# Evacuations one piece behind their products, B's additions on GpSimd, its transfers as single DMAs, and C's first sums in A's last rounds

**Chip, cores, metric.** One core of a Trainium2 chip. The metric is device time of one execution in microseconds (us); each quoted time is a median of several runs. The profile is of one such run. Engines: PE is TensorE, PEld its weight loads, DVE VectorE, ACT ScalarE, POOL GpSimd, SP the engine that issues the transfers.

## The reference

Four layers on x of shape 4 x 64 x 256 x 256, float32. Layers 0, 2 and 3 are long two-dimensional convolutions with a rank-one filter per channel; layer 1 goes to a Haar basis, mixes the channels, shrinks, and goes back.

```python
def _L0_conv_ref(x, ...):                       # also layers 2 and 3
    hx = _implicit_filter(z, Xw1, ...); hy = _implicit_filter(z, Yw1, ...)
    k = jnp.einsum('ijk,imk->ijmk', hx, hy)     # rank one: rows by columns
    y = irfft2(rfft2(x, 2L) * rfft2(k, 2L) / 2L)[..., :L, :L]
    return y + x * bias[:, None, None]

def _L1_conv_ref(x, v, conv_w, tau):
    f1 = haar2d(x)
    for i in range(2):
        f4 = jnp.einsum('bchw,oc->bohw', f1 * v[i], conv_w[i])
        acc = acc + jnp.sign(f4) * jax.nn.relu(jnp.abs(f4) - tau[i])
    return haar2d(acc, inverse=True) + x
```

## The kernel before

Because the filter has rank one, a convolution is two Toeplitz products (rows, then columns) on TensorE. The kernel has three phases, interleaved in program order:

- **A**: layer 0 and the forward Haar transform, 64 rounds of 12 pieces: 4 rows, 4 columns, 4 Haar products (of the round before). GpSimd does the sums of the other Haar direction. Results go to DRAM (`coef`).
- **B**: the mixing and shrinking, two groups of 128 units, each of three pieces (two units share one load of data); reads `coef`, `v`, `tau`, writes `mixed`. Group 0 lies beside the second half of A, group 1 beside the first half of C.
- **C**: the inverse Haar transform and layers 2 and 3, 64 rounds of 20 pieces.

Each engine works through its instructions in the order in which the pieces issue them. The parts that matter (cuts marked `...`):

```python
def rows(t, n):                                   # A; columns and product alike
    ps = bank(f"a1ps{n}_{t}")
    toeplitz(ps, s["x"][:, 2 * n : 2 * n + 2], s["toep"][n // NB], 0)
    s["y", n] = image("t0", f"ay{n}_{t}")
    nc.scalar.copy(s["y", n], ps)                 # evacuation, directly behind

# B: two PSUM pairs f4 in turn
def load(s):
    for g in range(2):                            # 64 partitions each
        part = slice(g * C, (g + 1) * C)
        nc.sync.dma_start(d["f"][part]..., coef[grp][:, rows]...)
        nc.sync.dma_start(d["v"][part]..., flat(v[rows]))
        nc.sync.dma_start(d["tau"][part]..., flat(taus[rows]))
def piece(u, j):
    if j == 0:   mix(u)              # PE     -> f4      (frees on threshold(u-2))
                 less(u - 1)         # DVE    |f4| - tau
    elif j == 1: multiply(u)         # DVE    f4 * v
                 sign(u)             # ACT
                 threshold(u - 1)    # DVE    max(., 0) * sign -> m, or -> f4 if u % 4 == 3
                 add(...)            # POOL   m + f;  then m + m on POOL, or m + f4 on DVE for odd s
    else:        magnitude(u)        # ACT

def beside(main, side, lead, tail):  # spreads the side pieces evenly, by number, over main
    ...
beside(a[:cut_a], rest, 2, 3 * M)              # rest: the filter networks of layers 2 and 3, ...
beside(a[cut_a:], phase_b(0), 5 * M, M)
beside(c[:cut_c], phase_b(1), 2 * M, 10 * M)   # C's first piece does the first loads and sums
beside(c[cut_c:], [], 0, 0)
```

## Time and profile before

3162.2 us (median of 4, 3160.7 to 3164.3). The prediction shows the busy times by stage, TensorE's floor in each and the waits. (A stage's floor is the time of its TensorE work at the full rate, as C shows it alone; what a stage takes beyond it is called lost.)

These lines of the page show who moves the data; the columns are the output and input, queue, count, KB of each, median us from issue to landing.

```profile
ft<-coef SPq DMA_DIRECT2D x256, 256.0 KB, 6.6
v<-in_v SPq DMA_DIRECT2D x256, 256.0 KB, 7.0
tau<-taus SPq DMA_DIRECT2D x256, 256.0 KB, 7.0
mixed<-gt SPq DMA_DIRECT2D x256, 256.0 KB, 6.0
```

Each of B's tensors takes two transfers of 64 partitions for every two units. These and the additions on two engines are what the change touches.

### The profile page before, as it was taken

The numbers are of one execution on the slowest core, as the hardware profiler recorded it, in microseconds if no ns is written. First come the engines' busy times: TensorE is split into PE (matmuls) and PEld (weight loads), VectorE is DVE, ScalarE is ACT, GpSimd is POOL, SyncE is SP. The second block draws the span as 40 slices with busy tenths as digits, with TensorE's granted clock in tenths as the row PEclk, the third lists the DMA queues.
The fourth block names the chain that finished last, engine by engine and source line by source line (L and its number), as shares of the span: only waits on it lengthen the run. The fifth ranks groups of instructions, "written<-read, shape, count | busy, mean of one in ns | idle before, by whom it ended". The sixth has DMA issues, their size and how long they took to land. (4 is left out here: it accounts for less than half of the span.)

```text
span 3159.3 us, 48195 instructions
## 1 busy us (share of the span) xinstructions
PE 2973.0 (94%) x17432; PEld 2535.1 (80%) x17432; DVE 1564.9 (50%) x1657; ACT 1230.2 (39%) x1799; POOL 1817.4 (58%) x2437
## 2 busy tenths in 40 slices
PE   5999999888988888599999999999999999999999
PEld 5989997666666666488877878887899999999998
DVE  2232213777777777457666667666732222222222
ACT  1333333444544445344444444444432222232222
POOL 2776675666766766655556555565664444444441
PEclk9999999999999999899999999999999999999999
DMA  6857898999999999789888988989744444444442
GB/s 159 215 179 193 226 234 226 258 274 272 274 275 270 274 277 265 230 195 268 233 244 226 250 231 238 249 226 255 205 141 132 141 124 124 124 138 132 127 120 87
DMA packets 380227, 656.76 MB, mean 208 GB/s; under 512 B 42134, under 2 KB 281399, under 8 KB 379992
## 3 DMA queue, kind: packets, MB, share of 16 engines
q1 hardware_dynamic: 379992, 653.69, 76.6%
q8 instruction: 140, 2.29, 0.3%
q14 instruction: 95, 0.78, 0.1%
HBM read 438.10 MB, written 215.42 MB: 207 GB/s over the span
## 5 line engine op out<-in xcount | busy, mean ns | idle before, releaser
L409 PE MATMUL f<-ft,mix_sb 128*128 128x512 f32 x1024 | 506.1, 617 | 112.6 <-DVE gt L438 57.3
L434 POOL TENSOR_TENSOR m<-m,ft 128x1024 f32<-128x1024 f32 x128 | 301.7, 2357 | 453.1 <-DVE m L429 441.4
L417 ACT ACTIVATE m<-f 128x1024 f32<-128x1024 f32 x256 | 262.5, 1025 | 513.1 <-DVE f L413 504.3
L546 DVE SCALAR_TENSOR_TENSOR cy<-cz,bias_sb,c1c 128x512 f32<-128x512 f32 x256 | 189.2, 746 | 515.9 <-PE c1c L224 515.9
L424 DVE TENSOR_TENSOR f<-f,tau 128x1024 f32<-128x1024 f32 x256 | 314.6, 1229 | 197.0 <-ACT f L420 194.2
L302 DVE SCALAR_TENSOR_TENSOR x<-x,bias_sb,a2ps 128x512 f32<-128x512 f32 x256 | 189.0, 745 | 428.8 <-PE a2ps L224 380.4
L409 PEld LDWEIGHTS f<-ft,mix_sb 128*128 128x128 f32 x1024 | 177.5, 193 | 258.3 <-issue 142.6
L546 DVE SCALAR_TENSOR_TENSOR o<-cy,bias_sb,c2c 128x512 f32<-128x512 f32 x256 | 189.5, 746 | 348.7 <-PE c2c L224 348.7
L413 DVE TENSOR_TENSOR f<-f,v 128x1024 f32<-128x1024 f32 x256 | 313.8, 1226 | 54.9 <-PE f L409 51.8
L223 PE MATMUL a1ps<-toep,x 128*128 128x256 f32 x1024 | 310.1, 385 | 21.3 <-DMA toep<-filt 18.1
L223 PE MATMUL a2ps<-toep,ay 128*128 128x256 f32 x1024 | 305.9, 381 | 1.8 <-ACT ay L292 1.8
L223 PE MATMUL c2r<-toep,cy 128*128 128x256 f32 x1024 | 305.8, 380 | 0.3 <-DVE cy L546 0.3
L223 PE MATMUL c1c<-toep,ch 128*128 128x256 f32 x1024 | 305.8, 380 | 0.0
L223 PE MATMUL c1r<-toep,cz 128*128 128x256 f32 x1024 | 305.8, 380 | 0.0
L223 PE MATMUL c2c<-toep,ch 128*128 128x256 f32 x1024 | 305.8, 380 | 0.0
L533 ACT COPY ch<-c2r 128x512 f32<-128x512 f32 x256 | 149.4, 588 | 382.4 <-PE c2r L224 382.2
L325 ACT ACTIVATE f<-a3ps,wcol_sb 128x512 f32<-128x512 f32 x256 | 175.7, 686 | 293.2 <-PE a3ps L317 251.5
L317 PEld LDWEIGHTS a3ps<-haarH_sb,fw 128*128 128x128 f32 x2048 | 244.9, 195 | 32.5 <-issue 22.7
L526 ACT COPY cz<-c1ps 128x512 f32<-128x512 f32 x256 | 148.1, 588 | 309.5 <-PE c1ps L522 309.5
L522 PEld LDWEIGHTS c1ps<-haarW_sb,ci 128*128 128x128 f32 x2048 | 238.8, 193 | 36.6 <-POOL ci L266 24.4
L522 PE MATMUL c1ps<-haarW_sb,ci 128*128 128x128 f32 x2048 | 244.6, 276 | 23.4 <-POOL ci L266 23.3
L420 ACT ACTIVATE f<-f 128x1024 f32<-128x1024 f32 x256 | 263.9, 1031 | 0.0
(64 smaller groups left out, 5868.5 us busy)
## 6 DMA issues: line engine op xcount, KB each, us to landing
toep<-filt SPq DMA_DIRECT2D x768, 128.0 KB, 4.1
x<-in_x SPq DMA_DIRECT2D x256, 256.0 KB, 7.8
coef<-f SPq DMA_DIRECT2D x128, 512.0 KB, 7.3
ft<-coef SPq DMA_DIRECT2D x256, 256.0 KB, 6.6
v<-in_v SPq DMA_DIRECT2D x256, 256.0 KB, 7.0
tau<-taus SPq DMA_DIRECT2D x256, 256.0 KB, 7.0
mixed<-gt SPq DMA_DIRECT2D x256, 256.0 KB, 6.0
g<-mixed SPq DMA_DIRECT2D x128, 512.0 KB, 5.4
```

What stands on the lines that cost most here:

```text
L223: nc.tensor.matmul(ps[:, m, :], data[:, 0, cut], t[:, which, :], start=True, stop=False)
L302: nc.vector.scalar_tensor_tensor(s["x1"][:, cut], s["x"][:, cut], bias_sb[:, c : c + 1], ps, ALU.mult, ALU.add)
L317: nc.tensor.matmul(ps[:, e, bass.ts(k, P)], s["fw"][:, 2 * (n + e) + k, bass.ts(m, P)], haarH_sb[:, k, :], start=True, stop=True,)
L325: nc.scalar.activation(f4[:, n : n + 2, m, :], ps, AF.Copy, scale=wcol_sb[:, m : m + 1])
L409: nc.tensor.matmul(un[u]["f4"][:, j, :], mix_sb[:, u % 2, :], f[:, j, :], start=True, stop=True)
L413: nc.vector.tensor_tensor(f4, f4, weights(st[u // 2]["v"], u % 2), ALU.mult)
L417: nc.scalar.activation(un[u]["m"], un[u]["f4"], AF.Sign)
L420: nc.scalar.activation(un[u]["f4"], un[u]["f4"], AF.Abs)
L424: nc.vector.tensor_tensor(f4, f4, weights(st[u // 2]["tau"], u % 2), ALU.subtract)
L434: nc.gpsimd.tensor_tensor(m0, m0, data(st[s]["f"]), ALU.add)
L522: nc.tensor.matmul(ps[:, m, bass.ts(h, P)], s["ci"][:, 2 * n + h, bass.ts(m, P)], haarW_sb, start=True, stop=True)
L546: nc.vector.scalar_tensor_tensor(o, s["y", n], bias_sb[:, at : at + 1], ps, ALU.mult, ALU.add)
```

## The change

Its intent: let no engine stand in front of an evacuation whose product is not done, take work and a PSUM wait off VectorE, move B's data in transfers of all 128 partitions, and fill the gap between A and C. Core of the diff (cut):

```diff
+    waiting = []
+    def later(op): waiting.append(op)
+    def flush():                    # called at the start of every piece of A and C
+        for op in waiting: op()
+        waiting.clear()
...
-            nc.scalar.copy(s["y", n], ps)
+            later(lambda: nc.scalar.copy(y, ps))          # the other five evacuations alike
...
-            for g in range(2): ... two DMAs of 64 partitions for f, v and tau each
+            nc.sync.dma_start(d["f"]..., rows_of(coef[grp], r0))   # partition = 2 * channel + g
+            for name, src in (("v", v), ("tau", taus)):
+                flat = bass.AP(src.tensor, ..., [[0, C], [C * 2 * W, 2], [1, ROWS * 2 * W]])
+                nc.sync.dma_start(d[name]..., flat)
...
-            o = un[u]["f4"] if u % 4 == 3 else un[u]["m"]
-            nc.vector.scalar_tensor_tensor(o, ...)
+            nc.vector.scalar_tensor_tensor(un[u]["m"], ...)
-                if s % 2: nc.vector.tensor_tensor(data(st[s]["g"]), m0, un[2 * s + 1]["f4"], ALU.add)
-                else:     nc.gpsimd.tensor_tensor(...)
+                nc.gpsimd.tensor_tensor(data(st[s]["g"]), m0, un[2 * s + 1]["m"], ALU.add)
...
-    beside(a[cut_a:], phase_b(0), 5 * M, M)
-    beside(c[:cut_c], phase_b(1), 2 * M, 10 * M)
+    beside(a[cut_a : -6 * M], phase_b(0), 5 * M, 0)           # B ends two rounds before A
+    beside(a[-6 * M : -2 * M], c_first[:1], 2 * M, M)         # C's first loads
+    beside(a[-2 * M :], c_first[1:], 0, 0)                    # C's first sums
+    main = a_last[:1] + c[:M]                                 # A's last sums; C's first products
+    for pair in zip(c[M : 2 * M], a_last[1:]): main += pair   # A's last products between C's rows
+    main += a_last[M + 1 :] + c[2 * M : cut_c]
+    beside(main, phase_b(1), 5 * M, 10 * M)
```

The mixing matrix and the fix of B's first row are rewritten for the new order of partitions.

More of the change, by code (lines that the diff above doesn't have):

```diff
@@ L68, in conv_haar_kernel @@
 def conv_haar_kernel(
-    ctx: ExitStack, tc: tile.TileContext, x, zT, w1, wbd, cols, decay, bias, haarW, haarH, wcol, wrow, mixT, v, tau, out
+    ctx: ExitStack, tc: tile.TileContext, x, zT, w1, wbd, cols, decay, bias, haarW, haarH, wcol, wrow, mixT, first, v, tau, out
 ):
@@ L198, in conv_haar_kernel @@
     mix_sb = const.tile([P, 2, P], F32, tag="mix", name="mix_sb")
-    nc.gpsimd.memset(mix_sb, 0.0)
-    for i in range(2):
-        for g in range(2):
-            s = slice(g * C, (g + 1) * C)
-            nc.sync.dma_start(mix_sb[s, i, s], mixT[i])
+    nc.sync.dma_start(mix_sb, mixT)
+    first_sb = const.tile([P, 2], F32, tag="first", name="first_sb")
+    nc.sync.dma_start(first_sb, first)
     def load_toeplitz(l, t, bufs):
@@ L269, in inverse_free, with later @@
             half *= 2
+    waiting = []
+    def later(op):
+        waiting.append(op)
+    def flush():
+        for op in waiting:
+            op()
+        waiting.clear()
     def run(ops, count):
@@ L290, in rows @@
             toeplitz(ps, s["x"][:, 2 * n : 2 * n + 2], s["toep"][n // NB], 0)
-            s["y", n] = image("t0", f"ay{n}_{t}")
-            nc.scalar.copy(s["y", n], ps)
+            y = s["y", n] = image("t0", f"ay{n}_{t}")
+            later(lambda: nc.scalar.copy(y, ps))
         def columns(t, n):
@@ L301, in columns @@
             cut = slice(2 * n, 2 * n + 2)
-            nc.vector.scalar_tensor_tensor(
-                s["x1"][:, cut], s["x"][:, cut], bias_sb[:, c : c + 1], ps, ALU.mult, ALU.add
+            later(
+                lambda: nc.vector.scalar_tensor_tensor(
+                    s["x1"][:, cut], s["x"][:, cut], bias_sb[:, c : c + 1], ps, ALU.mult, ALU.add
+                )
             )
@@ L324, in product @@
             f4 = s["f"].rearrange("p (n m) k -> p n m k", m=2)
-            nc.scalar.activation(f4[:, n : n + 2, m, :], ps, AF.Copy, scale=wcol_sb[:, m : m + 1])
+            dst = f4[:, n : n + 2, m, :]
+            later(lambda: nc.scalar.activation(dst, ps, AF.Copy, scale=wcol_sb[:, m : m + 1]))
         def coarsest(t):
@@ L342, in piece @@
         def piece(t, j):
-            now, last = t < total, t > 0
+            flush()
             if j == 0:
@@ L349, in piece @@
             if j < M:
-                if now:
-                    rows(t, j)
-                if last:
+                rows(t, j)
+                if t > 0:
                     run(st[t - 1]["ops"], 2)
             elif j < 2 * M:
-                if now:
-                    columns(t, j - M)
+                columns(t, j - M)
                 if j == M and t > 1:
@@ L361, in piece @@
             else:
-                if last:
+                if t > 0:
                     product(t - 1, j - 2 * M)
-                if now:
+                if t < total - 1:
                     run(st[t]["ops"], 2)
-        for t in range(total + 1):
+        for t in range(total):
             for j in range(3 * M):
                 pieces.append(lambda t=t, j=j: piece(t, j))
-        pieces.append(lambda: (coarsest(total - 1), store(total - 1)))
-        return pieces
+        t = total - 1
+        last = [lambda: (flush(), coarsest(t - 1), store(t - 1), run(st[t]["ops"], 16))]
+        last += [lambda j=j: (flush(), product(t, j)) for j in range(M)]
+        last.append(lambda: (flush(), coarsest(t), store(t)))
+        return pieces, last
     def phase_b(grp):
@@ L387, in load, with rows_of @@
             d["tau"] = bp.tile([P, ROWS, 2, W], F32, tag="tau", name=f"tau_{grp}_{s}", bufs=3)
-            for g in range(2):
-                part = slice(g * C, (g + 1) * C)
-                rows = slice(g * C + r0, g * C + r0 + ROWS)
-                flat = lambda ap: ap.rearrange("r i h k -> (r i h k)").partition_broadcast(C)
-                nc.sync.dma_start(
-                    d["f"][part].rearrange("p r b w -> p (r b w)"),
-                    coef[grp][:, rows].rearrange("c r b h k -> c (r b h k)"),
-                )
-                nc.sync.dma_start(d["v"][part].rearrange("p r i w -> p (r i w)"), flat(v[rows]))
-                nc.sync.dma_start(d["tau"][part].rearrange("p r i w -> p (r i w)"), flat(taus[rows]))
+            nc.sync.dma_start(d["f"].rearrange("p r b w -> p (r b w)"), rows_of(coef[grp], r0))
+            for name, src in (("v", v), ("tau", taus)):
+                flat = bass.AP(src.tensor, src.offset + r0 * 2 * W, [[0, C], [C * 2 * W, 2], [1, ROWS * 2 * W]])
+                nc.sync.dma_start(d[name].rearrange("p r i w -> p (r i w)"), flat)
+        def rows_of(ap, r0):
+            return ap.rearrange("c (g r) b h k -> c g r (b h k)", g=2)[:, :, r0 : r0 + ROWS].rearrange(
+                "c g r e -> c g (r e)"
+            )
         def data(t):
@@ L426, in threshold @@
         def threshold(u):
-            o = un[u]["f4"] if u % 4 == 3 else un[u]["m"]
-            nc.vector.scalar_tensor_tensor(o, un[u]["f4"], 0.0, un[u]["m"], ALU.max, ALU.mult)
+            nc.vector.scalar_tensor_tensor(un[u]["m"], un[u]["f4"], 0.0, un[u]["m"], ALU.max, ALU.mult)
         def add(s, which):
@@ L436, in add @@
                 st[s]["g"] = bp.tile([P, ROWS, NB, W], F32, tag="gt", name=f"gt_{grp}_{s}", bufs=3)
-                if s % 2:
-                    nc.vector.tensor_tensor(data(st[s]["g"]), m0, un[2 * s + 1]["f4"], ALU.add)
-                else:
-                    nc.gpsimd.tensor_tensor(data(st[s]["g"]), m0, un[2 * s + 1]["m"], ALU.add)
+                nc.gpsimd.tensor_tensor(data(st[s]["g"]), m0, un[2 * s + 1]["m"], ALU.add)
         def store(s):
@@ L445, in store @@
             if r0 == 0:
-                top = gt[:C, 0].rearrange("p b (h k) -> p b h k", h=2)
-                sd = bp.tile([C, NB, 2, N], F32, tag="sd", name=f"sd_{grp}", bufs=1)
-                nc.vector.tensor_tensor(sd[:, :, 0, :], top[:, :, 0, :], top[:, :, 1, :], ALU.add)
-                nc.vector.tensor_tensor(sd[:, :, 1, :], top[:, :, 0, :], top[:, :, 1, :], ALU.subtract)
-                nc.vector.tensor_copy(top, sd)
-            for g in range(2):
-                part = slice(g * C, (g + 1) * C)
-                rows = slice(g * C + r0, g * C + r0 + ROWS)
-                nc.sync.dma_start(
-                    mixed[grp][:, rows].rearrange("c r b h k -> c (r b h k)"), gt[part].rearrange("p r b w -> p (r b w)")
-                )
+                top, low = (gt[:, 0].rearrange("p b (h k) -> p b h k", h=2)[:, :, h, :] for h in range(2))
+                d = bp.tile([P, NB, N], F32, tag="sd", name=f"sd_{grp}", bufs=1)
+                one, sign_ = first_sb[:, 0:1], first_sb[:, 1:2]
+                nc.vector.tensor_scalar(d, top, one, None, ALU.mult)
+                nc.vector.scalar_tensor_tensor(top, low, one, top, ALU.mult, ALU.add)
+                nc.vector.scalar_tensor_tensor(low, low, sign_, d, ALU.mult, ALU.add)
+            nc.sync.dma_start(rows_of(mixed[grp], r0), gt.rearrange("p r b w -> p (r b w)"))
             st[s].clear()
@@ L524, in product @@
                     )
-            s["y", n] = image("t0", f"cz{n}_{t}")
-            nc.scalar.copy(s["y", n], ps)
+            y = s["y", n] = image("t0", f"cz{n}_{t}")
+            later(lambda: nc.scalar.copy(y, ps))
         def rows(t, l, n):
@@ L531, in rows @@
             toeplitz(ps, s["y", n], s["toep"][l - 1][n // NB], 0)
-            s["half", n] = image("t1", f"ch{l}{n}_{t}")
-            nc.scalar.copy(s["half", n], ps)
+            y = s["half", n] = image("t1", f"ch{l}{n}_{t}")
+            later(lambda: nc.scalar.copy(y, ps))
         def columns(t, l, n):
@@ L545, in columns @@
                 o = image("t2", f"cy{n}_{t}")
-            nc.vector.scalar_tensor_tensor(o, s["y", n], bias_sb[:, at : at + 1], ps, ALU.mult, ALU.add)
+            old = s["y", n]
+            later(lambda: nc.vector.scalar_tensor_tensor(o, old, bias_sb[:, at : at + 1], ps, ALU.mult, ALU.add))
             s["y", n] = o
@@ L556, in piece @@
         def piece(t, j):
+            flush()
             stage, n = divmod(j, M)
             if j == 0:
-                if t == 0:
-                    load(0)
-                    load(1)
-                    sums(0)
-                    run(st[0]["ops"], 16)
-                    filters(0)
                 filters(t + 1)
@@ L577, in piece, with start @@
                 run(st[t + 1]["ops"], 1)
+        def start():
+            load(0)
+            load(1)
+            filters(0)
+            sums(0)
+        first = [start] + [lambda: run(st[0]["ops"], 2)] * 8
         for t in range(total):
@@ L581, in phase_c @@
                 pieces.append(lambda t=t, j=j: piece(t, j))
-        pieces.append(lambda: store(total - 1))
-        return pieces
+        pieces.append(lambda: (flush(), store(total - 1)))
+        return first, pieces
     def beside(main, side, lead, tail):
@@ L593, in beside @@
             done = max(done, want)
-    a, c = phase_a(), phase_c()
+    (a, a_last), (c_first, c) = phase_a(), phase_c()
     cut_a, cut_c = ROUNDS * 3 * M, ROUNDS * 5 * M
@@ L600, in conv_haar_kernel @@
     bps = pool("bps", 2, space=PSUM)
-    beside(a[cut_a:], phase_b(0), 5 * M, M)
-    beside(c[:cut_c], phase_b(1), 2 * M, 10 * M)
+    beside(a[cut_a : -6 * M], phase_b(0), 5 * M, 0)
+    beside(a[-6 * M : -2 * M], c_first[:1], 2 * M, M)
+    beside(a[-2 * M :], c_first[1:], 0, 0)
+    main = a_last[:1] + c[:M]
+    for pair in zip(c[M : 2 * M], a_last[1:]):
+        main += pair
+    main += a_last[M + 1 :] + c[2 * M : cut_c]
+    beside(main, phase_b(1), 5 * M, 10 * M)
     beside(c[cut_c:], [], 0, 0)
@@ L662 @@
     haarW[0] *= math.sqrt(0.5)
+    mix = np.zeros((C, 2, 2, C, 2), np.float32)
+    for g in range(2):
+        mix[:, g, :, :, g] = a["L1_conv_conv_w"].transpose(2, 0, 1)
+    odd = np.arange(P) % 2
     arrays = {
@@ L690 @@
         "wrow": f(w[order].astype(np.float32)),
-        "mixT": f(a["L1_conv_conv_w"].transpose(0, 2, 1)),
+        "mixT": f(mix.reshape(P, 2, P)),
+        "first": f(np.stack([1.0 - odd, 2.0 * odd - 1.0], axis=1).astype(np.float32)),
         "v": by_row(v),
```

## The prediction

> **What bounds the kernel now.** I read, in this order, the page's busy shares, the busy time by stage (cut at 37 us, where the first product starts; at 522, where B's first load is issued; at 1321, A's last product; at 1343, C's first; at 2371, 32 rounds of C before the end), the waits of TensorE inside the stages, then the timeline. Columns of the stage view: stretch, its us, busy us (instructions) of PE, PEld, DVE, ACT, POOL, then granted clock, DMA share, GB/s.
>
> ```profile
> PE 2973.0 (94%) x17432; PEld 2535.1 (80%) x17432; DVE 1564.9 (50%) x1657; ACT 1230.2 (39%) x1799; POOL 1817.4 (58%) x2437
> ...
> 37.00:522.00 485.00, 479.64 (x3231) 449.60 (x3231) 120.06 (x164) 169.11 (x268) 336.24 (x625) 1.00 0.78 213
> 522.00:1321.00 799.00, 689.07 (x3444) 517.02 (x3442) 574.18 (x539) 384.35 (x504) 531.78 (x685) 0.97 1.01 264
> 1321.00:1343.00 22.00, 0.09 (x1) 0.09 (x1) 0.00 (x0) 0.64 (x1) 11.96 (x21) 0.61 0.89 276
> 1343.00:2371.00 1028.00, 1014.59 (x5640) 834.38 (x5641) 670.43 (x675) 448.64 (x640) 597.08 (x624) 1.00 0.85 228
> 2371.00:3159.00 788.00, 784.39 (x5114) 731.63 (x5113) 191.30 (x257) 224.90 (x384) 339.86 (x480) 1.00 0.42 125
> ```
>
> TensorE bounds it, so I need its floor per piece. In the chain of waits C's second half repeats with a period of 24.53 us a round: 32 Haar products take 3.57 us, and each pair of Toeplitz products (256 and 128 columns) 0.655 us, 32 of them 20.96. So an A round (rows, columns, product) has a floor of 5.24 + 5.24 + 3.57 = 14.05 us, and one of B's 256 units (two mixing products in four records) 1.72 us. Whole floor: 64 x 14.05 + 64 x 24.53 + 256 x 1.72 = 2909 us.
>
> Stage by stage: A alone until 522 is 33.67 rounds less one product, floor 469, took 485. A with B's first group: the rest of A (430) and 128 units (220), floor 650, took 799: **149 us lost**. The hand-over from A to C: 22 us with TensorE empty. C with B's second group: 785 + 220 = 1005, took 1028: 23 lost. C alone: nothing lost. So this is about the second stage and the hand-over. Who is waited for there:
>
> ```profile
> PE f L409 <- DVE gt L438: 45.7, 29, 3.5
> PE f L409 <- DVE m L429: 35.0, 35, 2.7
> PE f L409 <- DMA ft<-coef: 4.2, 3, 1.6
> ```
>
> (560 to 1290 us; total us, times, longest.) TensorE waits almost only before B's mixing product: its two-bank PSUM pair is free when VectorE has thresholded the unit two before (L429), or, for every fourth unit, has added it (L438, in order behind GpSimd's first addition). The idle records give 110 of the 149 us; the rest I put down to the lower granted clock (0.97) and refilling after each gap. Why VectorE is late, from the timeline:
>
> ```profile
> 906.15 0.75 DVE L302 SCALAR_TENSOR_TENSOR x<-x,bias_sb,a2ps 128x512 f32<-128x512 f32 x1 [2.24 <-PE a2ps L224]
> 906.82 1.22 DVE L413 TENSOR_TENSOR f<-f,v 128x1024 f32<-128x1024 f32 x1
> 907.95 1.21 DVE L429 SCALAR_TENSOR_TENSOR m<-f,m 128x1024 f32<-128x1024 f32 x1
> ...
> 909.22 1.98 PE L409 MATMUL f<-ft,mix_sb 128*128 128x512 f32 x4 [1.79 <-DVE m L429]
> ```
>
> The multiplication's input was ready at about 904.8 (mixing product at 902.82, 1.98 long), yet VectorE sat 2.24 us in front of A's evacuation, which waited for its own product; TensorE then waited 1.79 us (PE's own record) for the threshold at the end of that queue. The evacuation blocks the queue just when VectorE has B's work to do.
>
> **What the Trainium skill says.** "PSUM — Partial Sum Buffer", section "Engine vs sequencer instructions": ScalarE's, VectorE's and GpSimd's queues are strict FIFO. The lines above agree: 2.24 us lost with a ready instruction behind. "SBUF — State Buffer", section "Door 1: The DMA port swizzle": partitions 0..63 or 64..127 alone reach 8 of 16 ports, with an asymptote of about 218 GB/s. The trace agrees: the packet records of B's first loads (64 partitions each) show about 315 ns per 4 KB, at 218 GB/s, against 159 ns for A's 128-partition stores just before.
>
> ```profile
> 524.00:550.00 26.00, 19.92 (x88) 14.34 (x89) 10.50 (x11) 8.96 (x12) 11.20 (x20) 0.87 1.04 218
> ```
>
> "GPSIMD Engine Reference", section "3.1 Elementwise": an addition is 1.96 times slower on GpSimd at 2048 elements; here 2357 ns against 1221 at 1024, a ratio of 1.93. "SBUF — State Buffer", section "SBUF: two separate sides": GpSimd shares a port lock with VectorE operations of two SBUF inputs. B's and the evacuations' VectorE operations take one input from PSUM, and GpSimd's addition stays between 2339 and 2378 ns, so I count no slowing from the moved additions.
>
> **The change part by part.**
>
> 1. *Evacuations one piece behind.* Count unchanged: VectorE 0.745 us, ScalarE 0.59 to 0.69 each. They reach the queue when their product is done, so the 2 us blockings go. What then limits a unit? In the new schedule B's 394 steps lie over 340 pieces of A, three steps a unit, so 2.59 pieces a unit: TensorE's period is 1.72 + 2.59 x 1.171 = 4.75 us on average, 5.1 beside rows or columns, 4.03 beside products. The dependency mix (1.97) -> multiply (1.23) -> threshold of the unit before (1.21) -> next mix runs in about 4.5 us (815.11 to 819.61 in the trace). It fits beside rows and columns, not beside products: 0.47 us x 1.55 units x 28.3 rounds = 21 us lost. Beside columns VectorE has 3.67 + 2.59 x 0.745 = 5.6 us a unit against 5.1: for a unit and a half per round, some 0.35 us x 28 = 10 us.
>
> 2. *Additions on GpSimd.* VectorE loses 64 x 1.221 = 78 us in all, GpSimd gains 64 x 2.357 = 151. The wait for L438 goes. GpSimd in the second stage then has 128 x 2.357 = 302, and 28.33 rounds of A's sums at 10.55 (the sum of the rows of L235 to L244 and L331 to L333 over 64) = 299: 601 us of a TensorE floor of 28.33 x 14.05 + 220 = 618. That is 97%, tight, but over a stage of some 650 it is 92%. Its lag builds up beside products (5.4 us a round by the same sums) and drains beside rows and columns; five buffers for m give three units, 14 us.
>
> 3. *Single DMAs.* Same bytes. With 16 ports they should go at 159 ns a packet. Off the path directly (few waits for data above), but B's first 24 loads took 29 us, so starting gets some 10 us better (I leave 5 of loss). It is also needed: 64 steps x 2.1 MB and 28.3 rounds x 2.62 MB are 208 MB, which in 654 us are 318 GB/s; the stage now runs at 271 with the DMA share at 1.04.
>
> 4. *C's first sums in A's last rounds.* The hand-over now costs the 22 us, and 9 more in A's last round:
>
> ```profile
> 1315.50 5.42 PE L317 MATMUL a3ps<-haarH_sb,fw 128*128 128x128 f32 x32 [9.02 <-POOL fw L235]
> 1342.91 5.37 PE L522 MATMUL c1ps<-haarW_sb,ci 128*128 128x128 f32 x32 [22.00 <-POOL ci L266]
> ```
>
> After: GpSimd still has C's first sums (11.7 us, rows of L264 and L266 over 64) and then A's last (10.5) in a row, while TensorE has 5.24 + 3.57 us before it needs the first and 3.57 + 1.31 more before it needs the second. With GpSimd about 3 us behind at the start I get waits of 6 and 6.5: 13 us in place of 31. B ends before A's last two rounds, which run at their floor, 28.
>
> 5. *Store's first row, the mixing matrix:* a few instructions of a microsecond; nothing.
>
> **The sum.** Start 37 + A alone 469 + 14 lost (as now, a little less) = 520. A with B: 618 + 21 + 10 + 5 = 654, to 1174. A's last two rounds: 29, to 1203. Hand-over waits 13, to 1216. C with B, with A's last product: 3.6 + 1005 + 8 lost (23 now; the same blocking is removed, the unit period of about 7.2 us is loose) = 1017, to 2233. C alone 785, last store 3: **3021 us**, 4.5% below 3161.6; I say 3020.
>
> **The rivals.**
> *GpSimd becomes the bound.* For: 97% of the floor, strict order, additions that wait for VectorE (131 us of waits for L429 between 560 and 1290). Against: those waits come from late thresholds, which part 1 brings forward. If 10% of the stage stays idle, it takes 667 to 670; if 15%, 707: 3035 to 3075.
> *The chain of B is the bound everywhere.* Latencies and interposed evacuations make a unit take 5.2 us instead of 4.75 on average: 131 x 5.2 = 681, 3050. For: only two PSUM pairs. Against: 4.5 us loops are seen.
> *The transfers become the bound.* If single DMAs gained nothing, 64 x 9.85 us (2.1 MB at 213 GB/s) plus 28.3 x 7 (2.62 MB at about 375, the best 5 us of the stage) would be 829 us: only the hand-over and C would gain, 3130 to 3195. Against: A's 128-partition stores already go at 159 ns.
> On the good side, with the whole stage at the floor of 618 and 5 of waits at the hand-over: 2980.
>
> **Range and chances.** The good side and the GpSimd rival span 2980 to 3075; 8 in 10 for 2985 to 3070. Faster by over 2% needs less than 3098: only the transfer rival, or two others together, prevents it: 0.93. Within 2%: 0.06. Slower: 0.01.
>
> **What would show it.** Right: between B's first load and A's last two rounds some 655 us; waits of the mixing product for VectorE down from 81 us to some 30, those left beside A's Haar products; no VectorE evacuation with 2 us of idle before it; GpSimd about 92% busy there and all 128 of B's second additions on it; packets of B's loads near 160 to 200 ns, over 300 GB/s; two waits on GpSimd of 5 to 8 us at the hand-over; C alone unchanged. Wrong: TensorE waiting for GpSimd's fw in every round, ScalarE's sign waiting for m (GpSimd's buffers), or waits for ft, v, tau (transfers).

## The result, and the profile after

3032.4 us (median of 4, 3030.3 to 3034.7) against 3162.2. The ratio is 0.9589, 95% interval 0.9573 to 0.9606. Here and below a ratio is the mean time of one kernel's fast runs over that of the other's of the same rounds, so not quite the ratio of the medians. The prediction was 3020, range 2985 to 3070.

First the busy shares of the page, then the stages of the kernel after, cut at the same events (531: B's first load; 1191: A's last two rounds begin; 1225: C's first product; 2244: C's second half):

```profile
PE 2949.6 (97%) x17432; PEld 2528.4 (83%) x17432; DVE 1489.4 (49%) x1593; ACT 1229.1 (41%) x1799; POOL 1968.6 (65%) x2500
...
35.00:531.00 496.00, 486.14 (x3232) 454.75 (x3232) 120.21 (x164) 169.31 (x268) 337.07 (x625) 0.99 0.76 209
531.00:1191.00 660.00, 632.05 (x3216) 475.75 (x3216) 527.12 (x499) 370.57 (x482) 575.29 (x660) 0.99 0.92 314
1191.00:1225.00 34.00, 28.45 (x196) 26.61 (x194) 5.97 (x8) 11.06 (x18) 31.34 (x55) 0.96 0.52 187
1225.00:2244.00 1019.00, 1012.94 (x5665) 836.87 (x5666) 635.10 (x642) 450.59 (x644) 684.27 (x679) 1.00 0.68 233
2244.00:3033.00 789.00, 785.14 (x5121) 732.42 (x5119) 192.09 (x257) 225.05 (x384) 340.40 (x480) 1.00 0.42 125
```

From B's first load to C's first product it was 821 us and is 694: the whole gain is there. C with B is 8 us shorter, A alone 10 us *longer*. Beside B's first group DMA runs at 314 GB/s with a share of 0.92, where it ran at 264 with 1.01. The waits of TensorE over the whole span (total us, times, longest):

```profile
PE f L424 <- DVE m L442: 25.3, 36, 3.6
...
PE c1ps L528 <- POOL ci L266: 5.7, 1, 5.7
PE a1ps L223 <- ACT f L339: 4.5, 1, 4.5
PE a2ps L223 <- ACT ay L303: 4.5, 2, 2.8
PE a3ps L330 <- POOL fw L235: 3.9, 2, 3.6
```

The wait for the addition's line is gone, that for the threshold has become small, and the hand-over is two waits (5.7, and 3.6 of the 3.9). The two lines with ACT, all before B's first load, are 9.0 us, where the kernel before had 5.0; the prediction did not have that. VectorE's evacuations beside B no longer wait for their product: between 531 and 1191 us the profile shows 0.8 us of such waits, where the kernel before had 65.7 between 560 and 1290.

### The profile page after: what moved, and what is told of

Same layout as the page of the kernel before. It is cut to its first block, busy times and chain, and to the rows that moved or that the text cites. A ratio compares the mean times of both kernels' runs of the same rounds, so it can differ in the third digit from the quotient of the medians.

```text
span 3032.9 us, 47710 instructions
## 1 busy us (share of the span) xinstructions
PE 2949.6 (97%) x17432; PEld 2528.4 (83%) x17432; DVE 1489.4 (49%) x1593; ACT 1229.1 (41%) x1799; POOL 1968.6 (65%) x2500
## 4 chain that ended last, share of the span: by engine, by line
PE 79%; DVE 5%; POOL 3%; issue 2%; DMA 2%; ACT 1%; SPq 0%; POOLq 0%; DVEq 0%; ACTq 0%
PE f L424 12%; PE c1c L223 7%; PE c1r L223 7%; PE c1ps L528 7%; PE c2r L223 7%; PE c2c L223 7%; PE a1ps L223 4%; PE a2ps L223 4%; PE c1c L224 4%; PE c1r L224 4%; PE c2r L224 4%; PE c2c L224 4%; PE a3ps L330 3%; PE a1ps L224 2%; DVE f L428 2%
## 5 line engine op out<-in xcount | busy, mean ns | idle before, releaser
L424 PE MATMUL f<-ft,mix_sb 128*128 128x512 f32 x1024 | 490.5, 601 | 29.1 <-DVE m L442 25.3
L450 POOL TENSOR_TENSOR gt<-m,m 128x1024 f32<-128x1024 f32 x128 | 302.8, 2365 | 177.2 <-DVE m L442 117.5
L442 DVE SCALAR_TENSOR_TENSOR m<-f,m 128x1024 f32<-128x1024 f32 x256 | 310.7, 1214 | 0.1
L264 POOL TENSOR_TENSOR i<-g 128x8 f32<-128x8 f32 x64 | 14.3, 223 | 389.3 <-DMA g<-mixed 389.3
L435 ACT ACTIVATE f<-f 128x1024 f32<-128x1024 f32 x256 | 263.2, 1028 | 0.0
```

The source lines that it names most:

```text
L424: nc.tensor.matmul(un[u]["f4"][:, j, :], mix_sb[:, u % 2, :], f[:, j, :], start=True, stop=True)
L435: nc.scalar.activation(un[u]["f4"], un[u]["f4"], AF.Abs)
L442: nc.vector.scalar_tensor_tensor(un[u]["m"], un[u]["f4"], 0.0, un[u]["m"], ALU.max, ALU.mult)
L450: nc.gpsimd.tensor_tensor(data(st[s]["g"]), m0, un[2 * s + 1]["m"], ALU.add)
```

## The experiments

Twelve kernels; all gave correct results. "Stage" is the time from B's first load to the start of A's last two rounds, 660 us in the changed kernel. The kernel before took 3164 to 3165 us in these lots. The changed kernel itself was not run in them, so differences of a few us from its 3032.4 are judged by the ratios.

| run | edit | us | ratio to before |
|---|---|---|---|
| (the change) | | 3032.4 | 0.9589 |
| after_evac_now | without the deferral | 3086.3 | 0.9754 |
| before_evac_later | the deferral alone | 3151.8 | 0.9967 |
| after_two_dmas | two half transfers, in turn | 3067.1 | 0.9698 |
| after_two_dmas_old_order | two half transfers, the old order | 3129.5 | 0.9884 |
| after_two_row_dmas | two full-width transfers | 3030.4 | 0.9566 |
| after_adds_dve | odd additions back on VectorE | 3077.0 | 0.9722 |
| after_old_handover | the old hand-over | 3031.9 | 0.9575 |
| after_old_handover_dense | the same, B packed as in the change | 3051.5 | 0.9638 |
| after_flush_mlp | evacuations ahead of the network | 3026.2 | 0.9553 |
| after_by_time | B's steps laid out by time | 3029.0 | 0.9565 |
| after_mlp_by_time | the last two together | 3021.7 | 0.9542 |
| after_old_handover_mlp_time | all three | 3024.1 | 0.9548 |

### Are the evacuations the cause?

`after_evac_now`: deferral undone in the changed kernel.

```diff
     def later(op):
-        waiting.append(op)
+        op()
```

> The changed kernel with the evacuations of A and C issued at once again, directly behind their products; all else as changed. Theory (the evacuations waiting for their own product block VectorE's and ScalarE's queues, and that was most of the 149 us lost beside B's first group): the stage between B's first load and A's last two rounds grows from 660 to 720 to 750 us, the time from 3032 to 3080 to 3115 us, and VectorE again shows evacuations with 2 us of idle in front of them. The stretch before B gets some 10 us shorter (the network's layers). Rival (the gain came from the moved additions and the single transfers): under 3050 us.

Measured 3086.3 us. The stage is 713 us, and A alone is 10 us shorter again. VectorE waits for A's column products (first line, 560 to 1180 us), and TensorE for the threshold (second line, whole span):

```profile
DVE x L314 <- PE a2ps L224: 44.8, 51, 1.6
...
PE f L424 <- DVE m L442: 72.2, 73, 4.1
```

So the deferral is worth 54 us of the final time, and the mechanism is the predicted one: with 45 us of VectorE in front of unfinished products, TensorE waits 47 us more in front of its PSUM pair. In size the expectation was too high: the stage was to be 720 to 750 us, the single wait 2 us, and the longest is 1.6.

`before_evac_later`: the same deferral put into the kernel before, nothing else (`later` and `flush` as in the diff above).

> The kernel before with the evacuations one piece behind, and nothing else of the change. Theory (evacuations are the main cause of the waits, but transfers of 64 partitions at half rate are a second lid just above): the transfers of the stage, 214 MB at the 275 to 280 GB/s that the kernel before reaches at best over 20 us or more, need about 765 to 780 us, so only 20 to 35 us come off the 799 us, and 10 us are lost in the stretch before B: 3135 to 3155 us, with waits for ft, v or tau showing up on TensorE or VectorE. Rival A (transfers are no lid): the stage falls to 700 to 720 us, 3080 to 3100 us. Rival B (evacuations do not matter): 3160 to 3175 us.

Measured 3151.8 us, only 12 less. TensorE now waits for data, from 560 to 1180 us:

```profile
560.00:1180.00 620.00, 531.29 (x2667) 399.11 (x2666) 448.78 (x421) 297.99 (x391) 413.74 (x525) 0.97 1.03 267
...
PE f L424 <- DMA ft<-coef: 52.6, 22, 5.4
PE f L424 <- DVE gt L453: 17.3, 17, 2.0
...
530.00:1338.00 808.00, 689.55 (x3441) 518.82 (x3440) 574.35 (x539) 383.12 (x503) 532.50 (x685) 0.96 1.01 262
1359.00:2371.00 1012.00, 1008.54 (x5635) 832.44 (x5636) 671.53 (x675) 448.19 (x640) 598.38 (x624) 1.00 0.86 231
```

The waits for `ft` were 4.2 us in a longer window of the kernel before. With the evacuations out of the way, the limit is the DMA engines, which at a share of 1.03 move 267 GB/s. The last two lines are A with B's first group (B's first load to A's last product) and C with the second. The profile is of the slowest of the four executions (3161.7 us, 10 above the median); but even without those 10 us the first of the two stretches would be as long as in the kernel before (799 us). Of the 20 to 35 us that I expected there nothing is seen; what the deferral alone gains lies in C (1012 us against 1028). So in this stage of the kernel before the transfers were a limit as near as VectorE, although few waits there name them. Rival A, that transfers are no lid, falls.

### Is it the transfers, and what about them?

`after_two_dmas`: each of B's transfers as two, partitions 0 to 63 and 64 to 127.

```diff
-            nc.sync.dma_start(d["f"]..., rows_of(coef[grp], r0))
+            for q in (0, 1):
+                cs, ps_ = slice(q * 32, q * 32 + 32), slice(q * C, q * C + C)
+                nc.sync.dma_start(d["f"][ps_]..., rows_of(coef[grp], r0)[cs])
 # v, tau and mixed alike, tensor by tensor
```

> The changed kernel with each of B's four transfers cut in two again, channels 0 to 31 (partitions 0 to 63) and 32 to 63 (partitions 64 to 127); layout, bytes and packets unchanged. Theory (half of the ports, half of the rate, which the faster stage can no longer bear): the stage goes from 660 to 740 to 770 us, DMA share over 1.0 at 270 to 280 GB/s, 4 KB packets near 315 ns, waits of TensorE for ft or of VectorE for v and tau, time 3110 to 3145 us. Rival (the transfers are hidden anyway, the single DMAs only tidy up): under 3045 us.

Measured 3067.1 us: a loss of 35, well under what I expected (the stage is 702 us, not 740 or more). TensorE waits 33 us for `ft`, but the stage moves 299 GB/s (560 to 1180 us), more than I allowed for. So in this order the halves do not cost what they cost in the kernel before. Its order was another: all tensors of one half, then all of the other.

`after_two_dmas_old_order`:

```diff
+            for q in (0, 1):            # q outermost: f, v, tau of one half, then of the other
+                nc.sync.dma_start(d["f"][ps_]..., rows_of(coef[grp], r0)[cs])
+                for name, src in (("v", v), ("tau", taus)):
+                    nc.sync.dma_start(d[name][ps_]..., flat)
```

> As the run with two transfers of 64 partitions each, but in the order of the kernel before: coefficients, v and tau of the first 64 partitions, then those of the other 64. Same number of transfers, same bytes. Theory (what counts is that all transfers in flight go to the same half of the ports): slower than the alternating order, which took 3067 us: 3080 to 3130 us, 4 KB packets near 300 ns, DMA share at 1.03 or more with 270 to 290 GB/s in the stage. Rival (the number of transfers or their issue counts): the same as the alternating order, 3060 to 3072 us.

Measured 3129.5 us, 97 more than the change (stage 760 us), with the same number of transfers as the run before it. The upper lines are the old order's stage and its wait for data over the whole span; below them B's first loads, before A's transfers mix in, in the single form (533 to 547 us of the changed kernel):

```profile
560.00:1180.00 620.00, 549.79 (x2648) 405.05 (x2646) 443.77 (x417) 308.62 (x400) 478.25 (x546) 0.95 1.04 277
...
PE f L425 <- DMA ft<-coef: 65.8, 23, 5.1
```

```profile
533.00:547.00 14.00, 12.67 (x61) 9.24 (x62) 6.71 (x6) 6.52 (x9) 8.88 (x16) 1.00 0.99 360
```

`after_two_row_dmas`: two transfers again, but all 128 partitions in each, cut along the row.

```diff
+            for q in (0, 1):
+                e = slice(q * W, q * W + W)
+                nc.sync.dma_start(d["f"]...[:, e], rows_of(coef[grp], r0)[:, :, e])
```

> The changed kernel with each of B's transfers cut in two along the row and not along the partitions: 128 partitions each, 2 KB packets, same bytes, twice the number of transfers and issues. Theory (ports, not number): 3028 to 3042 us, as the changed kernel. Rival (number of transfers or the time to issue them): 3055 to 3075 us, as with two transfers of 64 partitions.

Measured 3030.4 us, the same as the change. So it is not that there are fewer transfers, or that they take less time to issue: it is that each covers all 128 partitions. (Each packet here has 2 KB and takes a median of 84 ns in the first loads, so 4 KB take about as long as in one transfer.) The packet records of B's first loads agree: 4 KB take a median of 159 ns in the changed kernel and 315 in the old order of halves, and the rate is 360 against 223 GB/s. In those first loads the alternating halves reach 232 GB/s, 4% more than the old order; the Trainium skill, "SBUF — State Buffer", section "Can I just issue two DMAs to hit both halves?", measured 6% for two such transfers at once, which is close. Why alternating then costs 35 us and the old order 97 is not settled. Between 560 and 1180 us, where A's transfers run beside B's, the 4 KB packets take a median of 180 ns with alternation, 238 in the old order and 159 in the changed kernel, so there the two orders do differ in rate. But with alternation the coefficients, which TensorE needs first, also come before v and tau, and no run separates the two.

### The additions

`after_adds_dve`: every second of B's second additions back on VectorE, by the removed lines of the diff above.

> The changed kernel with every second of B's second additions back on VectorE (the threshold of every fourth unit written to PSUM, added from there). Theory (a smaller part of the gain: VectorE gets 39 us more in the stage and the PSUM pair of every fourth unit waits for GpSimd's first addition again): stage 675 to 700 us, time 3047 to 3072 us, waits of the mixing product for the addition's line back at 15 to 40 us. Rival A (GpSimd at 87% of the stage is the real bound): faster, 3010 to 3030 us. Rival B (the additions do not matter): 3027 to 3037 us.

Measured 3077.0 us, 45 more; stage 706 us. I expected 15 to 40 more and at most 700. The wait is back:

```profile
PE f L424 <- DVE gt L452: 42.7, 33, 2.8
PE f L424 <- DVE m L443: 17.9, 24, 1.6
```

The addition runs in order behind GpSimd's first addition, and TensorE's PSUM pair is held until it is done. Together the two waits are 35 us more than the 25.3 of the changed kernel. How much of that is the held pair, and how much the 39 us of work more on VectorE, no run separates. GpSimd has less to do here, and the kernel is slower: GpSimd is not the bound of the changed kernel.

### The hand-over

`after_old_handover`: A's last product, then C's first loads and sums, then C; B spread to A's end (373 pieces instead of 340).

```diff
-    beside(a[cut_a : -6 * M], phase_b(0), 5 * M, 0)
-    ... c_first in A's last rounds, a_last in C's first
+    beside(a[cut_a:] + a_last, phase_b(0), 5 * M, M)
+    for q in c_first: q()
+    beside(c[:cut_c], phase_b(1), 2 * M, 10 * M)
```

> The changed kernel with the hand-over from A to C in the order of the kernel before: A's last product and store first, then C's first loads and sums, then C; B's first group spread to A's end again. Theory (the hand-over is worth what its two waits shrank by, 31 us in the kernel before against 9.3 us in the changed one, less a little because B's steps lie less densely): TensorE empty again for 20 us or more before C's first product and for some 9 us in A's last, time 3045 to 3056 us. Rival (the overlap only moves the wait into A's last rounds and C's first): 3027 to 3038 us.

Measured 3031.9 us: no loss at all, against my expectation. Yet the waits of the hand-over are back; it is B's that have gone:

```profile
PE c1ps L528 <- POOL ci L266: 21.8, 1, 21.8
...
PE a3ps L330 <- POOL fw L235: 11.6, 2, 11.3
PE f L424 <- DVE m L442: 8.9, 12, 2.9
```

To free A's last two rounds for C's sums, the change packs B into fewer pieces of A, so TensorE comes round to the next mixing product sooner and waits more for VectorE: 25.3 us against 8.9. If that is the reason, the old hand-over with the dense packing must show both losses.

`after_old_handover_dense`:

```diff
-    beside(a[cut_a:] + a_last, phase_b(0), 5 * M, M)
+    beside(a[cut_a:] + a_last, phase_b(0), 5 * M, 37)     # 340 pieces, as in the change
```

> The changed kernel with the old hand-over, and with B's first group packed into the same 340 pieces of A as in the changed kernel (the old hand-over alone, with B's steps spread to A's end over 373 pieces, took 3032 us, no more than the changed kernel). Theory (the new hand-over saves some 24 us of waits and gives them back by packing B more densely): with the dense packing the waits of the mixing product are back at some 25 us and those of the hand-over stay at some 33: 3048 to 3060 us. Rival (the new hand-over saves nothing by itself, or loses elsewhere in C): 3028 to 3040 us.

Measured 3051.5 us, with both:

```profile
PE f L424 <- DVE m L442: 24.2, 35, 3.6
PE c1ps L528 <- POOL ci L266: 21.3, 1, 21.3
```

So the hand-over by itself is worth 19 us (15 by the ratios), and the packing that makes room for it costs about as much (20 us between the last two runs).

### The loss before B, and the waits that are left

`after_flush_mlp`: evacuations issued ahead of each piece beside A's first half.

```diff
-    beside(a[:cut_a], rest, 2, 3 * M)
+    beside(a[:cut_a], [lambda q=q: (flush(), q()) for q in rest], 2, 3 * M)
```

> The changed kernel with the held-back evacuations issued ahead of every piece of the filter network (and of the other steps beside A's first half). Theory (the changed kernel lost some 10 us before B's first load, because a held-back evacuation on ScalarE or VectorE is issued behind a whole layer, with its chain on VectorE and a sine that waits for it, so that TensorE runs out of inputs and then at half clock): first product to first load of B from 495 back to about 486 us, time 3020 to 3026 us. Rival (the 10 us have another cause, such as the transfers' order or the start): 3030 to 3035 us.

The changed kernel at the third layer of the network, ScalarE and then TensorE; TensorE of the edited kernel at the same place; and TensorE of `after_adds_dve`, whose first half of A is that of the changed kernel:

```profile
200.96 0.63 ACT L151 ACTIVATE h<-u 128x512 f32<-128x512 f32 x1 [6.98 <-DVE u L149]
201.49 2.03 ACT L303 COPY ay<-a1ps 128x512 f32<-128x512 f32 x4
...
202.11 1.22 PE L223 MATMUL a2ps<-toep,ay 128*128 128x256 f32 x2 [2.76 <-ACT ay L303]
203.13 0.64 PE L224 MATMUL a2ps<-toep,ay 128*128 128x128 f32 x2
```

```profile
199.99 0.70 PE L223 MATMUL a2ps<-toep,ay 128*128 128x256 f32 x2 [1.46 <-ACT ay L303]
200.53 0.38 PE L224 MATMUL a2ps<-toep,ay 128*128 128x128 f32 x2
```

```profile
201.19 0.70 PE L223 MATMUL a2ps<-toep,ay 128*128 128x256 f32 x2 [2.76 <-ACT ay L303]
```

In the changed kernel four evacuations lie behind a sine that waits 7 us for VectorE; TensorE runs dry for 2.76 us, and its products then take longer (1.22 us for the first two instead of 0.70) for some 6 us, at a granted clock of 0.50 between 202 and 208 us. The Trainium skill, "TensorE: Matmul & The Clock Gate", section "What's actually happening", describes this: an idle TensorE falls to half its clock and needs sustained work to get it back. Issued earlier, the evacuations leave a wait of 1.46 us and the clock stays up. The stretch before B falls from 495 to 486 us, the time to 3026.2. The intervals of the two ratios (0.9540 to 0.9566; 0.9573 to 0.9606) do not touch.

The other traces show that the wait is the cause and the clock an addition that varies. Eight more kernels here hold the evacuations back in this stretch and have the same 2.76 us of idle; in only two of them the clock falls after it, in the other six it stays at 1.00 (third fence: the first two products take 0.70 us). From TensorE's first product to its 34th round the kernel before takes 473.3 us, the four variants of the changed kernel without evacuations held back behind the network 473.5 to 474.3, the seven others 478.6 to 480.8, and the profiled execution of the changed kernel, the slowest of its four (3034.7 us), 483.1. So 5 to 8 us are usual, and its 10 are more than usual. In `after_by_time` the same edit takes off 7 us (3029.0 to 3021.7, below).

`after_by_time`: B's steps laid out by the time of A's pieces.

```diff
-            want = len(side) * max(0, k + 1 - lead) // max(1, len(main) - lead - tail)
+            spent = sum(cost(i) for i in range(lead, k + 1)); want = len(side) * spent // total
 # cost: 131 for A's rows and columns, 89 for its Haar products; 1 elsewhere
```

> The changed kernel with B's steps in A's second half laid out by the time of A's pieces (131 for rows and columns, 89 for Haar products) and not by their number. Theory (the waits that are left stand beside the Haar products, where TensorE comes round in 4.0 us and the chain of mixing, multiplication and threshold takes 4.5): a period of 4.75 us everywhere, the waits of the mixing product fall from 24 us to 10 or less, stage 645 to 655 us, time 3017 to 3027 us. Rival (VectorE's load beside the columns or GpSimd's 87% is what limits the stage): 3030 to 3045 us, with the waits moved to the columns.

Measured 3029.0 us. Of the waits for the threshold 16.4 us are left of 25.3. By the timeline of the changed kernel they had stood behind Haar products (16.3 us) or the rows just after them (7.5); now it is 5.5 and 4.1, with 5.8 behind the columns, where it had been 0.3. So it was the right place, but the remedy moves a third of the waits to the columns, as the rival said. The ratio's interval (0.9552 to 0.9578) overlaps that of the change: a gain is not shown.

`after_mlp_by_time`: both edits.

> The changed kernel with both of the two edits above. They touch different stages, so the gains should add: 3006 to 3020 us if both theories hold, 3020 to 3026 if only the first, 3017 to 3027 if only the second.

Measured 3021.7 us, ratio 0.9542 (0.9529 to 0.9555): the lowest time, clear of the change's interval. But it lies in the range that I gave for the first edit alone, and the interval overlaps that of `after_flush_mlp`: that the second edit adds to it is not shown.

`after_old_handover_mlp_time`: these two with the old hand-over.

> A try for the best version: old hand-over with B spread to A's end, evacuations issued ahead of the network's pieces, B's steps laid out by time. The first is worth nothing by itself, the second 6 us; the third was worth 3 to 5 us with the dense packing and should be worth less here, where only 9 us of waits are left: 3020 to 3027 us, against 3021.7 for the best so far.

Measured 3024.1 us, ratio 0.9548: level with the best. Waits for the threshold are down to 4.6 us, and 34 us of hand-over stand against it.

## Why the prediction was right, point by point

*The bound, and evacuations blocking VectorE's queue:* right for the changed kernel, and half of the truth for the kernel before. Undone, the waits and 54 us come back; but the deferral alone does not shorten A beside B, because the half-width transfers were a limit just as near. That TensorE's idle records name VectorE did not mean that VectorE alone was the bound. In the lines at 906 us, too, the multiplication was ready only from 904.80 on, so 1.35 of the 2.24 us were lost with a ready instruction behind. *VectorE's evacuations without 2 us of idle before them:* right (0.8 us in the stage).

*Transfers: "also needed":* right; "off the path directly" holds only as long as the evacuations are in the way. The rival's sum for half-rate transfers gave "3130 to 3195", and the run with the old order took 3129.5, but that is luck in part: its stage was to be 829 us and was 760, at 275 GB/s, where the sum has some 251. Of the parts undone one at a time this costs most, although the kernel before showed almost no wait for data. The packets went from about 315 to 159 ns, as forecast. The parts do not add: undone one at a time, deferral, transfers and additions cost 54, 97 and 45 us, more together than the 130 gained. Single transfers or moved additions alone in the kernel before were not run.

*Additions on GpSimd:* the removed wait is right; GpSimd was 87% busy in the stage, not 92. The work was nearly as forecast (the records add up to 596 us, against 601), but neighbouring records overlap, and the busy time of 575 us counts the overlap once. It is not the bound, as said.

*The stage beside B, 654 us:* measured 660. The 21 us beside the Haar products are about right (16.3 us of waits there and 7.5 just behind). The 10 us beside the columns did not appear (0.3 us); by its own figures (5.6 against 5.1 us, a unit and a half a round) that term should have been about 21, so the sum was wrong as well. The 5 us of start are a wait of 3.3. What the sum lacked is some 14 us that are no idle record: 42 lost, 28 of them idle. That 654 came so near is therefore partly luck: a term too many and a term missing.

*The hand-over: 13 us in place of 31:* measured 9.3, with 22.0 and 9.0 before. The term is right; what I missed is that it is no net gain, because the denser packing it needs costs as much. My sum contained that cost under the stage, without naming where it came from.

*A alone: "14 lost (as now, a little less)":* **the term that failed.** It was 26 in the profiled execution, because deferred evacuations got stuck behind the network's layers, and in that trace this makes up most of the 12 us by which 3020 was too low. By the medians it is about half: with that mended the time is 3026.2.

*C with B, with A's last product, 1017 us:* measured 1019, of which 3.6 are the hand-over's second wait. *C alone:* unchanged.

## What to carry to other kernels

An instruction that waits for another engine holds up everything behind it in its queue: issue evacuations a piece late where other work on that engine feeds the bottleneck, but flush them before a long chain of another kind. A resource at the edge of its rate can show hardly any waits (here 4.2 us, at a DMA share of 1.04) and still hold the stage as soon as the other limit is gone, so work out what the faster stage will demand of it; and make each transfer span all 128 partitions. When a gap is filled by packing other work more densely, price the packing too: the 15 to 19 us of the hand-over went that way.

## What the Trainium skill lacked or had wrong

- "SBUF — State Buffer", section "Can I just issue two DMAs to hit both halves?", says that two half transfers serialize. B's first loads agree (232 against 223 GB/s), but in the loaded stage the order of the halves mattered by 62 us (3067 against 3129). The page has nothing on such an order.
- The same page, section "Door 1: The DMA port swizzle", gives rates but not how a half-width transfer looks in a trace: 4 KB packets at about 315 instead of 159 ns, and a DMA share of 1.04 at 218 GB/s, where B's first loads over all 128 partitions show 0.99 at 360. A full share does not mean a full rate.
- "TensorE: Matmul & The Clock Gate", section "What's actually happening", puts the drop after an idle window of about 3.4 us. Here less was enough at times: in the nine traces with 2.76 us of idle at the network's third layer the clock fell to 0.50 in three, for 3 to 7 us; after the 4.55 us at the next layer it fell in all nine; after the 3.24 us of the five traces without the held-back evacuations it fell in two. The length of the idle time alone did not decide it.
